# A graph attention kernel picks rows for 352 of 512 places of a chunk instead of 256

## Chip, core and metric

The kernel runs on one core of one Trainium2 chip. The metric is the device time of one execution in microseconds. Five engines work in parallel, each through its own queue in order: TensorE (PE, with its weight loads as PEld), VectorE (DVE), ScalarE (ACT), GpSimd (POOL), and SyncE (SP), which here only issues transfers.

## The reference

A graph of 6250 nodes with 64 features and 206,250 edges sorted by destination goes through three layers of transformer convolution, each edge carrying 64 features of its own:

```python
def _transformer_conv(x, src, dst, edge_attr, Wq, bq, Wk, bk, Wv, bv, We, Ws, bs):
    q = x @ Wq + bq
    kj = (x @ Wk + bk)[src] + edge_attr @ We
    alpha = sum(q[dst] * kj, -1) / sqrt(64)
    w = softmax of alpha over the edges of each dst
    agg = segment_sum(((x @ Wv + bv)[src] + edge_attr @ We) * w[:, None], dst)
    return agg + x @ Ws + bs
```

Between layers stand a relu and a layer norm, after the last a relu and a log softmax; the output is the layer norm of the input plus that result. The sources are drawn at random, so `x[src]` reads rows in no order.

## The kernel before

The edges stand in 403 chunks of 512; a chunk is 4 tiles of 128 edges, and 4 chunks make a batch. A unit is the work on one batch; a layer has 102 of them. A unit needs, for each of its 2048 edges, the row of `x` of the edge's source and the edge's own features, side by side in a buffer `feat`. TensorE transposes `feat` (`turn`, L1525), multiplies with the queries to scores (L1536, L1538), DVE takes their maximum (L1545), ACT the exponential (L1552); the weights are transposed (L1564) and sum the rows of `feat` (L1577); SP stores the parts, which are later finished to nodes, four blocks of 128 nodes at a time.

**Gathers.** A source row comes to `feat` by an indirect transfer that POOL issues, 128 rows of 64 numbers each (`gather`). Those of later units are released in order by gates: ACT copies the column of indices into a buffer (L609), and POOL's transfer reads it from there (L610).

**Picks.** A part of the rows isn't gathered but picked. All nodes stay on the chip as `halves` (each number as a rounded part and its rest). Layer 0 moves the edges inside each chunk so that certain places hold only sources out of a known range of nodes. There are 8 ranges of `BW` = 6 blocks of 128 nodes, each with 32 places in a chunk, 256 places in all: two tiles. For a pair of ranges and 8 chunks (two batches) DVE compares the keys of the places with the numbers 0 to 767 (`aim`: six comparisons of 512 columns, L1216, into `hot`), and TensorE multiplies the blocks with the ones so found (`bank`: 2 x 6 matmuls of 256 columns, L1242). ACT copies the result into `kept` (L1249), four matmuls of 64 columns per chunk-tile set turn it to rows while adding part and rest (`naturals`, L1259), and DVE copies these into `feat` (L1276, L1278). The keys come from DRAM (`key`, L1200), one load of 1024 columns, spread to all partitions, for four pairs of ranges.

`PICKED = (1, 2, 2)` says how many of the four tiles are picked in layers 0, 1 and 2. So a unit of layer 0 gathers 12 tiles, a unit of layers 1 and 2 gathers 8. The first `LEAD` = 4 batches of layer 0 are not picked at all and gather 16.

**Layer 0** does the moving while it works on units that were moved before, four chunks per unit. Every fourth unit `mark` handles 16 chunks: it finds each edge's range, counts how many of a range stand ahead of it with matmuls against a triangle (L892), takes the first 32 of each range to their places and the others to the remaining places, in their old order. These steps are separate pieces of a generator, and one is done at each quarter of a unit. Then DVE makes one-hot rows of the new positions (`hit`, L1000) and TensorE moves the features and a stamp of the source with them (products, L1012 and L1021). Tile t of the moved edges needs the first `REACH[t]` columns at most, which is why those products are narrower than 512; `mark` also checks on the chip that this holds and that every place found an edge (`few`), and a general path stands ready if not. The `index` step turns the stamps into index columns (L1058, L1061) and keys. Results go to DRAM (`eaS`, `eaP`, `toS`, `keyS`) and are read back in layers 1 and 2.

**Order in layers 1 and 2.** One iteration u issues: store the parts of u - 2, scores of u - 1, one bank, the transposes of u with the requests of u + 1 between them (`ask` and `across`: `to`, `q` and `featT` on SP), the weights of u - 1, `naturals` in every second iteration, one more bank, the sums of u - 1. The tile pools set waits: two `key` buffers, six `hot` buffers, four `feat` buffers.

## Time and profile before

| | before |
|---|---|
| time, median of 3 runs | 4249.41 us (4247.88 to 4252.58) |
| time of the profiled execution | 4238.36 us |
| its span | 4236.3 us |
| mean granted clock of TensorE | 0.872 |
| busy: PE / PEld / DVE / ACT / POOL | 81% / 61% / 73% / 49% / 71% |
| gathers, layers 1 and 2 together (L610, `feat<-x`) | 1608 with a gate, mean 1061 ns |
| gathers, layer 0 (L610, `feat<-in_x`) | 1212 with a gate, mean 1056 ns |

The busy shares are averages over stages that differ. Layer 0 runs to about 1890 us, layer 1 from 1940 to about 3050, layer 2 from about 3100 to the end. The page of the profile has no chain of waits for this execution; what sets the time is read from each engine's busy time, from its idle gaps and what ended them, stage by stage. A row of windows gives the busy time of each engine with the number of instructions, then the granted clock, the DMA share and GB/s; a row of groups gives count, busy time and mean, and after the bar the idle time just before these instructions and what ended most of it.

### The profile page before, as it was taken

To read this page: it belongs to the slowest core of one execution; us is meant where nothing else is said; L and a number is where in the kernel's file an instruction comes from. 1 tells how busy PE (TensorE), PEld (TensorE's weight loads), DVE (VectorE), ACT (ScalarE), POOL (GpSimd) and SP (SyncE) were. 2 spreads that over 40 slices of the span, in tenths; PEclk is the share of its full clock that TensorE was granted. 3 is DMA by queue.
4 is the path that set the end of the run, shared out by engine and by line. 5 is a ranking of instruction groups with operands and counts; after the bars stand their busy time and mean duration, and the time that the engine had idled before them with its cause. 6 is when DMAs were issued, how large, how long until landed. Compare 5 with 4: busy or idle time off the path is not lost.

```text
span 4236.3 us, 105299 instructions
## 1 busy us (share of the span) xinstructions
PE 3428.8 (81%) x33967; PEld 2576.5 (61%) x33967; DVE 3083.3 (73%) x8792; ACT 2090.9 (49%) x6475; POOL 3019.6 (71%) x2863
## 2 busy tenths in 40 slices
PE   5678887887888787868888888888688888888886
PEld 3445555555555555546776677766467767676774
DVE  6667777777877788856777777777567777777775
ACT  2345555455555555553455545455435555555554
POOL 5457777777776777756777777777567777777775
PEclk9889998999998999987888889889778888888887
DMA  7567777777777778854666767666546666666664
GB/s 164 153 168 201 212 199 192 202 204 199 200 212 200 195 208 214 223 158 113 161 170 172 170 162 171 160 170 169 136 111 165 161 172 163 170 165 164 164 167 105
DMA packets 749709, 737.56 MB, mean 174 GB/s; under 512 B 390960, under 2 KB 501578, under 8 KB 749150
## 3 DMA queue, kind: packets, MB, share of 16 engines
q1 hardware_dynamic: 565854, 510.70, 47.3%
q0 software_dynamic: 91264, 93.64, 12.0%
q10 hardware_dynamic: 92032, 126.38, 8.6%
q8 instruction: 276, 4.52, 0.5%
q14 instruction: 283, 2.32, 0.2%
HBM read 570.27 MB, written 160.07 MB: 172 GB/s over the span
## 4 chain that ended last, share of the span: by engine, by line


## 5 line engine op out<-in xcount | busy, mean ns | idle before, releaser
L610 POOL DMA_INDIRECT feat<-x,gate x1608 | 1705.3, 1061 | 514.3 <-issue 250.2
L610 POOL DMA_INDIRECT feat<-in_x,gate x1212 | 1279.8, 1056 | 566.9 <-ACT gate L609 263.7
L1216 DVE TENSOR_SCALAR hot<-key,rank 128x512 fp32r<-128x512 f16 x2976 | 1244.9, 486 | 112.7 <-PE ps_x L1242 87.4
L1242 PEld LDWEIGHTS ps_x<-hot,halves 128*128 128x128 f32 x4800 | 705.4, 218 | 193.8 <-DVE hot L1216 71.0
L1242 PE MATMUL ps_x<-hot,halves 128*128 128x256 f32 x4800 | 811.4, 322 | 1.4 <-DVE hot L1216 0.2
L1528 ACT COPY featT<-ps_a 64x512 f32<-64x512 f32 x1192 | 691.1, 580 | 219.3 <-PE ps_a L1525 202.3
L1525 PE MATMUL ps_a<-ident,feat 128*128 128x128 f32 x2380 | 365.1, 280 | 262.0 <-DMA feat<-x,gate 261.9
L609 ACT COPY gate<-src_b 128x1 int32<-128x1 int32 x2772 | 454.2, 191 | 94.5 <-ACT eT L1035 41.0
L1577 PE MATMUL ps_g<-feat,probT 128*32 128x128 f32 x9672 | 423.0, 326 | 86.7 <-ACT probT L1567 39.2
L1525 PEld LDWEIGHTS ps_a<-ident,feat 128*128 128x128 f32 x2380 | 274.0, 143 | 351.8 <-issue 283.8
L1249 ACT CAST kept<-ps_x 128x512 fp32r<-128x512 f32 x400 | 234.3, 586 | 414.7 <-PE ps_x L1242 412.5
L1545 DVE TENSOR_REDUCE most<-ps_s 128x1 f32<-128x512 f32 x297 | 203.8, 686 | 314.8 <-PE ps_s L1538 311.3
L1012 PE MATMUL ps_x<-hit,rest 128*64 128x512 bf16 (+3 forms) x3200 | 426.5, 356 | 0.0
L1577 PEld LDWEIGHTS ps_g<-feat,probT 128*32 128x32 f32 x9672 | 315.4, 131 | 156.6 <-ACT probT L1567 52.3
L1000 DVE TENSOR_SCALAR hit<-ruler,pos 128x512 bf16<-128x512 f16 (+3 forms) x1600 | 410.3, 326 | 0.0
L1552 ACT ACTIVATE prob<-ps_s,part 128x512 f32<-128x512 f32 x297 | 204.4, 688 | 348.9 <-PE ps_x L1242 200.3
L1538 PE MATMUL ps_s<-featT,q 128*32 128x512 f32 x2376 | 318.0, 607 | 0.0
L1012 PE MATMUL ps_x<-hit,raw 128*64 128x512 bf16 (+3 forms) x1600 | 297.0, 367 | 7.0 <-DVE hit L1000 7.0
L1567 DVE COPY probT<-ps_p 128x512 f32<-128x512 f32 x204 | 139.2, 683 | 216.8 <-PE ps_p L1564 209.3
L1564 PE MATMUL ps_p<-ident,prob 128*128 128x128 f32 (+1 forms) x1224 | 212.6, 301 | 73.2 <-ACT prob L1552 59.2
L1012 PEld LDWEIGHTS <-rest 128*64 128x64 bf16 x3200 | 197.8, 120 | 97.0 <-issue 32.4
L1564 PEld LDWEIGHTS ps_p<-ident,prob 128*128 128x128 f32 (+1 forms) x1224 | 151.4, 153 | 114.6 <-ACT prob L1552 72.7
(239 smaller groups left out, 4381.2 us busy)
## 6 DMA issues: line engine op xcount, KB each, us to landing
feat<-eaP SPq DMA_DIRECT2D x296, 512.0 KB
featT<-eaS SPq DMA_DIRECT2D x296, 512.0 KB
key<-keyS SPq DMA_DIRECT2D x248, 256.0 KB
raw<-in_ea SPq DMA_DIRECT2D x200, 256.0 KB
eaS<-eT ACTq DMA_DIRECT2D x200, 256.0 KB
eaP<-eN ACTq DMA_DIRECT2D x200, 256.0 KB
feat<-x,gate POOLq DMA_INDIRECT x1608
part<-part SPq DMA_DIRECT2D x600, 32.5 KB
```

The source lines that it names most:

```text
L609: copy(gate, index[:, i + t : i + t + 1])
L610: nc.gpsimd.indirect_dma_start(out=loaded[layer, k][:, c, t, 0], out_offset=None, in_=xts[layer][:, :], in_offset=bass.IndirectOffsetOnAxi ...
L1000: nc.vector.tensor_scalar(hit, ruler[:, : REACH[t]], self.pos[:, at : at + 1], None, ALU.is_equal)
L1012: nc.tensor.matmul(self.px[i][j * D : (j + 1) * D, : REACH[t]], self.part(i, part)[:, (j * T + t) * D : (j * T + t + 1) * D], self.hits[t, ...
L1216: nc.vector.tensor_scalar(hot, self.keys[k, t][:, 2 * i * PAIR * W : 2 * (i + 1) * PAIR * W], rank[:, h : h + 1], None, ALU.is_equal,)
L1242: nc.tensor.matmul(px[:, cols], halves[b >= EARLY][:, b - EARLY * (b >= EARLY)].rearrange("p h d -> p (h d)"), made[h][:, cols], start=(h ...
L1249: nc.scalar.copy(kept[t][:, :, 2 * i : 2 * i + 2].rearrange("p c q e -> p q c e"), px.rearrange("p (q c e) -> p q c e", q=2, e=W),)
L1525: nc.tensor.transpose(pt[:, j - js[0], t // 2], rows[:, t * D : (t + 2) * D], ident)
L1528: nc.scalar.copy(featT[:, :, :, h, :], pt[h * D : (h + 1) * D])
L1538: nc.tensor.matmul(self.p_s[rows], self.q[:, j * STRIDE : j * STRIDE + W], self.featT[:, j, :], start=False, stop=True)
L1564: nc.tensor.transpose(p_t[:, t, :n], self.prob[:n, t * P : (t + 1) * P], ident[:n, :n])
L1577: nc.tensor.matmul(p_g[rows, :].rearrange("n (h d) -> n h d", h=2), self.probT[:, t, rows], batch[:, c + j, t], start=(t == 0), stop=(t == ...
```

## The change

The places of a chunk that are picked grow from 256 to 352, in layers 1 and 2 alone: two tiles and the first 96 rows (`PART`) of the third. In layer 0 still one tile of four is picked.

- **Ranges.** There are 22 ranges of 4 blocks with 16 places each. They overlap: range w covers blocks 2w to 2w + 3. A range is made of steps of two blocks (25 `BINS`), and each edge goes to the range that has room by a running count: the steps' counts are summed, limited by the capacity so far, and turned into a shift for each step, which two scans on DVE do (L922, L924).
- **`mark`.** Ten matmuls of 128 columns are replaced by 4 of 400 columns against ones, then 14 of 400 for the counts inside each step (in four pieces, last tile first), 25 of 64 columns that add up the steps, and 10 of 16 that count the edges not placed. The pieces grow from 8 to 11; DVE reads each of these results out of PSUM. The four transposes of the old place table (`pn`) stand in the new code twice, once as a piece of their own.
- **Reach.** The columns needed by tiles 0, 1 and 2 grow to 392, 416 and 456 (the fourth always has 512).
- **Picks.** A bank now covers a pair of ranges for 16 chunks (four batches): 4 comparisons of 512 columns and 2 x 4 matmuls of 256. Layers 1 and 2 have 11 such pairs in four units, staggered so that two or three fall on each unit; layer 0 has 4. The keys of each pair come by one or two loads of their own. There are three `key` buffers and, in layers 1 and 2, two sets of `hot` buffers (`later`) instead of one.
- **Gathers.** In layers 1 and 2 a batch gathers the fourth tile of each chunk and one shared tile, `spare`, with the last 32 rows of the third tile of the four chunks: 5 transfers instead of 8. ACT copies the four parts of `spare` into `feat` (`settle`). The `naturals` of a unit are done in every iteration, for two tiles and for the 96 rows.
- **Lead.** The first 8 batches of layer 0 are not picked, instead of 4.

```diff
-BW = 6
-BINS = 2 * LB
-QUARTERS = P // W
-PAIR = 2 * LB
-NP = BINS * BW
+BW = 4
+SL = 16
+WINDOWS = 22
+SLOTS = WINDOWS * SL
+BINS = 25
+PART = SLOTS - 2 * P
+REST = P - PART
+TURN = 4
 GC = 16
 ROWS = 8
 STRIDE = W // 2
 BACK = 8
-PICKED = (1, 2, 2)
-LEAD = 4
-REACH = (288, 320, 416, CH)
+PAIRS = (P // (2 * SL), WINDOWS // 2, WINDOWS // 2)
+LEAD = 8
+REACH = (392, 416, 456, CH)
...
+    def rows_wanted(layer, k):
+
+        m = batches[k][1]
+        if not placed(layer, k):
+            return [(c, t) for c in range(m) for t in range(T)]
+        if not layer:
+            return [(c, t) for c in range(m) for t in range(1, T)]
+        return [(None, 0)] + [(c, T - 1) for c in range(m)]
+
...
+    def take(layer, k, c, t, index):
+
+        nc.gpsimd.indirect_dma_start(
+            out=spares[layer, k] if c is None else loaded[layer, k][:, c, t, 0],
+            out_offset=None,
+            in_=xts[layer][:, :],
+            in_offset=bass.IndirectOffsetOnAxis(ap=index, axis=0),
+        )
...
+    def settle(layer, k):
+
+        if layer and placed(layer, k):
+            for c in range(LB):
+                nc.scalar.copy(
+                    loaded[layer, k][PART:, c, 2, 0], spares[layer, k][c * REST : (c + 1) * REST, :]
+                )
 
...
+        those = rows_wanted(layer, k)
+        pending.extend((layer, k, c, t, k * LB + i * LB / len(those)) for i, (c, t) in enumerate(those))
...
-        nc.vector.tensor_tensor(lh, lh, ge[:, 1:], ALU.subtract)
-        yield
-        pc = ps("a")
-        sofar = pc[:, : BINS * n].rearrange("p (h c t) -> p h c t", h=BINS, t=T)
-        kinds = lh.rearrange("p h (c t) -> p h c t", t=T)
-        for t in range(T):
-            for i in range(t + 1):
-                nc.tensor.matmul(
-                    sofar[:, :, :, t], ones if i < t else tri, kinds[:, :, :, i], start=(i == 0), stop=(i == t)
-                )
...
+            kinds.rearrange("p h c t -> p h (c t)"),
+            half.unsqueeze(1).to_broadcast([P, BINS + 1, n]),
+            slab.unsqueeze(2).to_broadcast([P, BINS + 1, n]),
+            ALU.is_equal,
+        )
+        pc = ps("a")[:, : m * BINS]
+        for t in range(T):
+            nc.tensor.matmul(
+                pc.rearrange("p (c h) -> p h c", h=BINS), ones, kinds[:, :BINS, :, t], start=(t == 0), stop=(t == T - 1)
+            )
+        below, lift = [counts[:, i] for i in range(2)]
+        flat = "p c h -> p (c h)"
+        nc.vector.tensor_tensor_scan(below, carry[:, :m].rearrange(flat), pc, 0.0, ALU.mult, ALU.add)
+        yield
+        nc.vector.tensor_tensor_scan(lift, climb[:, :m].rearrange(flat), below, 0.0, ALU.add, ALU.max)
+        nc.vector.scalar_tensor_tensor(lift, below, float(SL), lift, ALU.add, ALU.subtract)
+        lift = lift.rearrange("p (c h) -> p c h", h=BINS)
+        nc.vector.tensor_reduce(few[:, 1, g : g + 1], lift[:, :, : BINS - 1], AX.XY, ALU.min)
+        nc.vector.tensor_tensor(lift, lift, shift.unsqueeze(1).to_broadcast([P, m, BINS]), ALU.add)
+        yield
+        for t in reversed(range(T)):
+            pc = ps("a")[:, : m * BINS].rearrange("p (h c) -> p h c", h=BINS)
+            for i in range(t + 1):
+                nc.tensor.matmul(pc, ones if i < t else tri, kinds[:, 1:, :, i], start=(i == 0), stop=False)
+            nc.tensor.matmul(
+                pc, ones[0:1, :], lift[0:1].rearrange("p c h -> p h c"), start=False, stop=True
+            )
+            nc.vector.tensor_tensor(kinds[:, 1:, :, t], pc, kinds[:, 1:, :, t], ALU.mult)
+            yield
+        pc = ps("a")[:, :n]
+        for h in range(BINS):
+            nc.tensor.matmul(
+                pc, same, kinds[:, 1 + h].rearrange("p c t -> p (c t)"), start=(h == 0), stop=(h == BINS - 1)
+            )
...
+        at = pc.rearrange(by, t=T)
+        for t in range(T):
+            for i in range(t + 1):
+                nc.tensor.matmul(
+                    at[:, :, t], ones if i < t else tri, kinds[:, 0, :, i], start=(i == 0), stop=(i == t)
+                )
...
+        pn = ps("a")
+        w0 = r0 // W * W
+        w = min(W, NC - k * P - w0)
+        place = pn[:, : T * w].rearrange("p (t c) -> p c t", t=T)[:, r0 - w0 : r0 - w0 + m]
+        for t in range(T):
+            nc.tensor.transpose(
+                pn[:, t * w : (t + 1) * w],
+                start[w0 : w0 + w, k * CH + t * P : k * CH + (t + 1) * P],
+                ident[w0 : w0 + w, w0 : w0 + w],
...
+            pk = pa[:LB, W : W + SLOTS]
+            nc.tensor.matmul(pk, keyc, self.to[:, :SLOTS], start=True, stop=True)
+            for t in range(1, T):
+                nc.tensor.matmul(
+                    pi[:, 1 + (t - 1) * LB : 1 + t * LB], self.to[:, t * P : (t + 1) * P], pickc, start=True, stop=True
+                )
+            for c in range(LB):
+                nc.tensor.matmul(
+                    pi[c * REST : (c + 1) * REST, 0:1], self.to[:, SLOTS : 3 * P], pickc[:, c : c + 1], start=True, stop=True
+                )
...
+            low = 0 if layer else U0
+            self.jobs = []
+            for k in range(low - TURN + 1, NT):
+                for q in range(PAIRS[layer]):
+                    if q % TURN == k % TURN:
+                        self.jobs.append((k, max(k, low), min(k + TURN, NT), q))
...
+            while self.loads and len(self.keys) < 3:
+                _, k0, k1, q = job = self.loads[0]
+                if not self.layer and not coded.issuperset(range(k0, k1)):
                     return
+                key = picks.tile([P, TURN * LB * 2 * SL], FP16, name="key", bufs=3)
+                n = LB * 2 * SL
+                while k0 < k1:
+                    m = min(k1 - k0, TURN - k0 % TURN)
+                    nc.sync.dma_start(
+                        key[:, k0 % TURN * n : (k0 % TURN + m) * n],
+                        keyS[q, k0 : k0 + m].rearrange("k c e -> (k c e)").partition_broadcast(P),
+                    )
+                    k0 += m
...
+            if not self.aims or self.aims[0] not in self.keys or len(self.hots) > (self.layer > 0):
                 return
+            job = self.aims.pop(0)
+            a, b = self.span(job)
+            pool = later if self.layer and self.aimed % 2 else picks
+            self.aimed += 1
             made = []
...
+                    block = 2 * (2 * q + w) + h
+                    assert halved[block] == self.layer
                     nc.tensor.matmul(
+                        px[:, w, a:b],
+                        halves[block >= EARLY][:, block - EARLY * (block >= EARLY)].rearrange("p h d -> p (h d)"),
+                        made[h][:, a:b, w],
...
+            found = loaded[self.layer, k]
+            for ts, tag in (((0, 1), tags[0]), ((2,), tags[1])) if self.layer else (((0,), tags[0]),):
+                n = P if ts[0] < 2 else PART
+                pn = ps(tag)[:n, : len(ts) * LB * D].rearrange("p (t c d) -> p t c d", t=len(ts), d=D)
+                for t in ts:
                     for c in range(LB):
...
-                picker.bank()
-                drip(u)
+                picker.naturals(u + 1, "mp")
+                picker.bank(u + 2)
                 close_up(3) if close else step()
-                this.turn(0, lambda: drip(u))
+                this.turn(0, lambda: drip(u, 0.5))
                 ask(layer, u + 1)
                 chunks[layer, u + 1].across()
                 this.turn(1, lambda: drip(u, 0.5))
                 close_up() if close else step()
                 line.weights(u)
                 close_up(3) if close else step()
-                if u % 2:
-                    picker.naturals(u + 1, "ms")
-                picker.bank()
+                while picker.due(u + 2):
+                    picker.bank(u + 2)
                 drip(u)
                 picker.load()
                 line.sums(u)
                 free(u, LB - 1)
+                settle(layer, u + 1)
...
-            if odd:
-                picker.bank("g")
+            picker.naturals(u + 1, "p")
+            picker.bank(u + 2, "g")
...
-            for _ in range(PICKED[layer + 1] * QUARTERS // 2):
-                picker.bank()
-            picker.naturals(0, "ms")
-            picker.bank()
+            while picker.due(0):
+                picker.bank(0)
+            picker.naturals(0, "mp")
+            settle(layer + 1, 0)
+            while picker.due(1):
```

TensorE in an iteration of layers 1 and 2, from the scores to the sums (`ps_x` is a bank, `ps_m`, `ps_s` and `ps_p` with `twice` are the naturals, `ps_a` the transposes). Before:

```order
L1538 MATMUL ps_s<-featT,q 32x512 x4
L1242 MATMUL ps_x<-hot,halves_31087 128x256 x12
L1525 MATMUL ps_a<-ident,feat 128x128 x8
L1564 MATMUL ps_p<-ident,prob 128x128 x4
L1259 MATMUL ps_m<-twice,kept_254 128x64 x4
L1259 MATMUL ps_m<-twice,kept_31088 128x64 x4
L1259 MATMUL ps_s<-twice,kept_254 128x64 x4
L1259 MATMUL ps_s<-twice,kept_31088 128x64 x4
L1242 MATMUL ps_x<-hot,halves 128x256 x12
L1577 MATMUL ps_g<-feat,probT 32x128 x16
```

After:

```order
L1605 MATMUL ps_s<-featT,q 32x512 x4
L1338 MATMUL ps_m<-twice,kept_261 128x64 x4
L1338 MATMUL ps_m<-twice,kept_32321 128x64 x4
L1338 MATMUL ps_p<-twice,kept_32322 96x64 x4
L1314 MATMUL ps_x<-hot,halves 128x256 x8
L1592 MATMUL ps_a<-ident,feat 128x128 x8
L1631 MATMUL ps_p<-ident,prob 128x128 x4
L1314 MATMUL ps_x<-hot,halves_32320 128x256 x16
L1644 MATMUL ps_g<-feat,probT 32x128 x16
```

The naturals moved from behind the weights' transposes, for two units at a time in every second iteration, to the place right behind the scores, for one unit in each; the picks are 8 and 16 matmuls instead of 12 and 12.

SP in an iteration of layers 1 and 2. Before, from one unit's `to` to the next one's:

```order
L1473 DMA to_210<-toS 6x512 x4
L1478 TENSOR_LOAD base
L1487 REGISTER_ALU
L1487 DMA q<-qq 128x80
L1504 DMA featT<-eaS 64x4x512
L1200 DMA key<-keyS 128x1024
L559 DMA feat<-eaP 128x1024
L1591 ISA
L1591 DMA part_173<-part 64x130
L1591 ISA
L1591 DMA part_174<-part 64x130
```

After:

```order
L1257 DMA key<-keyS 128x384
L1257 DMA key<-keyS 128x128
L1540 DMA to_213<-toS 6x512 x4
L1545 TENSOR_LOAD base
L1554 REGISTER_ALU
L1554 DMA q<-qq 128x80
L1571 DMA featT<-eaS 64x4x512
L1257 DMA key<-keyS 128x384
L1257 DMA key<-keyS 128x128
L559 DMA feat<-eaP 128x1024
L1658 ISA
L1658 DMA part_176<-part 64x130
```

One load of 1024 columns became loads of 512 in one or two pieces, and some of them now stand ahead of `to`, `q` and `featT`.

DVE in layer 0, at the place where a `mark` begins its counting (`hit` and `rest` belong to the moving, `most` and `part` to the scores). Before:

```order
L879 TENSOR_TENSOR ge<-src_b,edges 128x576
L885 TENSOR_TENSOR ge<-ge 128x512
L1545 TENSOR_REDUCE most<-ps_s 128x1
L1547 TENSOR_SCALAR part<-most 128x1
L982 TENSOR_TENSOR rest<-raw 128x512
```

After:

```order
L909 TENSOR_TENSOR kinds<-misc,slab 128x1664
L922 SCALAR_TENSOR_TENSOR bins<-carry,ps_a 128x400
L1612 TENSOR_REDUCE most<-ps_s 128x1
L1614 TENSOR_SCALAR part<-most 128x1
L1345 COPY feat<-ps_p 128x4x64
```

The first scan (L922) reads TensorE's result `ps_a` and stands right behind the comparison that TensorE waits for, ahead of the scores' maximum; before, nothing of `mark` read PSUM on DVE at this place, since ACT copied the counts.

259 lines of the change are left out of this document (106 added, 153 removed).

## The prediction

> **What bounds the kernel now.** I read first the busy time of each engine by stage, where layer 0 is 400 to 1800 us and layer 1 is 2100 to 3000 (columns: busy us and instructions of PE, PEld, DVE, ACT, POOL, then granted clock and DMA).
>
> ```profile
> 400.00:1800.00 1400.00, 1134.49 (x12524) 763.88 (x12524) 1092.58 (x3560) 731.88 (x2249) 1018.42 (x969) 0.92 0.77 205
> 2100.00:3000.00 900.00, 773.60 (x7544) 629.10 (x7546) 676.11 (x1654) 459.60 (x1470) 699.74 (x657) 0.88 0.68 168
> ```
>
> Then the groups of layer 1, by form, and its longest waits.
>
> ```profile
> L610 POOL DMA_INDIRECT feat<-x,gate x657 | 700.6, 1066 | 200.6 <-issue 102.1 <-ACT gate L609 43.6 <-DMA feat<-x,gate 24.1
> L1216 DVE TENSOR_SCALAR hot<-key,rank 128x512 fp32r<-128x512 f16 x996 | 416.6, 486 | 35.6 <-PE ps_x L1242 30.1 <-DVE feat L1276 0.2
> L609 ACT COPY gate<-src_b 128x1 int32<-128x1 int32 x664 | 119.1, 192 | 0.0
> L1249 ACT CAST kept<-ps_x 128x512 fp32r<-128x512 f32 x166 | 97.2, 586 | 146.3 <-PE ps_x L1242 145.4
> ...
> PE ps_a L1525 <- DMA feat<-x,gate: 103.2, 56, 5.8
> ```
>
> In layers 1 and 2 POOL never rests. Busy time and gap of its gathers are 700.6 + 200.6 = 901 us of 900, 1.372 us per gather, and the longest named part of the gap is its own issue. Eight gathers make a batch of four chunks, so a unit takes 8 x 1.372 = 10.97 us (900 / 657 x 8 = 10.96). PE, the busiest of the others, is idle 126.4 us, and 103.2 us of that is the transposes at L1525 waiting for gathered rows. DVE is busy 8.24 us of a unit (676.1 / 82.1 units), ACT 5.6.
>
> Layer 0 is another machine.
>
> ```profile
> L1000 DVE TENSOR_SCALAR hit<-ruler,pos 128x512 bf16<-128x512 f16 x320 | 99.1, 370 | 0.0
> L1000 DVE TENSOR_SCALAR hit<-ruler,pos 128x288 bf16<-128x288 f16 x324 | 73.5, 286 | 0.0
> L892 PE MATMUL ps_a<-ge,ones 128*128 128x128 f16 x120 | 22.2, 297 | 0.0
> L901 DVE TENSOR_REDUCE spare<-ge 128x64 f32<-128x512 f16 x20 | 20.6, 1028 | 0.7
> L879 DVE TENSOR_TENSOR ge<-src_b,edges 128x576 f16<-128x576 int32 x20 | 14.9, 745 | 0.0
> L1545 DVE TENSOR_REDUCE most<-ps_s 128x1 f32<-128x512 f32 x80 | 55.2, 690 | 169.0 <-PE ps_s L1538 168.9
> ```
>
> L1545 runs once a unit: 80 units in 1400 us, 17.5 us each. PE is busy 14.2 of it, DVE 13.7, and POOL needs 12 gathers, 16.5 us at 1.372. Nothing is full; PE and DVE wait for each other in turn (DVE 169 us for the scores alone), so work added to PE's queue is mostly added to the unit.
>
> **Layers 1 and 2: three gathers fewer.** A batch takes 5 gathers, 5 x 1.372 = 6.86 us of POOL. POOL stops being the bound, and the next bound sets the gain. One iteration at full clock, the same after a stall, and the queue of SP:
>
> ```profile
> 2502.40 1.06 PE L1259 MATMUL ps_m<-twice,kept 128*128 128x64 f32 x8
> 2503.29 1.06 PE L1259 MATMUL ps_s<-twice,kept 128*128 128x64 f32 x8
> ...
> 2508.51 1.03 PE L1538 MATMUL ps_s<-featT,q 128*32 128x512 f32 x8
> 2509.47 1.69 PE L1242 MATMUL ps_x<-hot,halves 128*128 128x256 f32 x12
> 2511.01 1.03 PE L1525 MATMUL ps_a<-ident,feat 128*128 128x128 f32 x8
> ...
> 2522.59 0.45 PE L1525 MATMUL ps_a<-ident,feat 128*128 128x128 f32 x1 [2.61 <-DMA feat<-x,gate]
> ...
> 2526.96 2.91 PE L1242 MATMUL ps_x<-hot,halves 128*128 128x256 f32 x12
> ...
> 2514.91 1.41 SPq L1473 DMA_DIRECT2D to<-toS  x4
> 2517.11 0.38 SPq L1487 DMA_DIRECT2D q<-qq  x1
> 2517.55 0.66 SPq L1504 DMA_DIRECT2D featT<-eaS  x1
> 2518.46 0.39 SPq L1200 DMA_DIRECT2D key<-keyS  x1
> ...
> 2521.25 2.01 SPq L1473 DMA_DIRECT2D to<-toS  x4
> ```
>
> *PE.* Now 773.6 / 82.1 = 9.42 us a unit at a granted clock of 0.88. The picks take 22 matmuls a unit instead of 24 (11 banks of 8 for four units): 12 of them start 1.54 us apart (2509.47 to 2511.01), 0.128 each, so -0.26. Turning the picks into rows takes 12 matmuls instead of 8, at 0.89 / 8 = 0.111: +0.44. That gives 9.60 us at today's clock. If the clock rose to 1.0 and all of it followed, 9.60 x 0.88 = 8.45. With the idle time that is not the gathers', (126.4 - 103.2) / 82.1 = 0.28, the bounds are 8.73 and 9.88.
>
> *DVE.* 11 comparisons instead of 12, -0.42 (416.6 / 996), and a third copy of picked rows, 96x256, at most the same: still 8.24, near PE's lower bound.
>
> *ACT.* Banks 2.75 instead of 2 (+0.44 at 0.586), four small copies of the spare rows (+0.77 at 0.192 if priced like the gates), three gates fewer (-0.54 at 0.179): 6.3 us, under the others. These copies are a new wait: they stand at the end of an iteration and wait for the spare gather, with the next exponentials and gates queued behind them. The spare is the first gather of a batch, released two iterations ahead, so I cost the wait at nothing; without that cover every late gather would stop ACT for up to the 5.8 us above.
>
> *SP.* From `to` to `to` SP's issues of one unit take 6.34 us. Keys come in 19 DMAs for four units instead of 4, 3.75 more a unit at about 0.45 with the gap before each: +1.7, about 8.0, before what finishing nodes adds. A key load also waits until the comparisons that free its buffer are done, and one now stands ahead of the next `to`, `q` and `featT`, which were ahead of it. featT is loaded an iteration before its scores, which should cover that.
>
> So the unit lands between 8.7 and 9.9 us. With PE, DVE and SP all at 8 to 9.6 and each waiting for the others, I take a value toward the upper end, **9.6 us**. Some 97 units a layer: 194 x (10.96 - 9.6) = **-264 us** (bounds -433 and -210; -154 if SP stretches it to 10.2).
>
> **Layer 0: a wider sort and a dearer rank pass.**
>
> ```profile
> 1028.64 1.67 PE L1242 MATMUL ps_p<-hot,halves 128*128 128x256 f32 x12
> 1030.24 0.33 PE L1012 MATMUL ps_x<-hit,raw 128*64 128x320 bf16 x2
> ...
> 1031.92 0.44 PE L1021 MATMUL ps_m<-hit,stamp 128*32 128x320 bf16 x8
> ```
>
> *Products.* 24 matmuls of 304 columns on average fill 1030.24 to 1031.92, 0.23 ns a column. The reaches grow by 104, 96 and 40 columns; twelve matmuls each: 12 x 240 x 0.23 = +0.66 us a unit. The stamps (0.44 us for 8 of 304: 0.18 ns) add 4 x 240 x 0.18 = +0.17. Picks: 8 matmuls instead of 12 at 1.60 / 12 = 0.133, -0.53. The index step has a few small matmuls more, +0.1.
>
> *Rank pass*, once in four units. Ten 128-column matmuls at 0.185 (22.2 / 120) go, -1.85. There come 18 of 400 columns, 35 small ones and four transposes, which stand in the code twice. No row has a 400-column one: the pick's 256 in 0.133 give 0.21, L892 scaled by columns 0.58. I take 0.21, since L892's pitch is that of its weight loads: 3.8 us. The small ones go at 0.111: 3.9. The transposes 0.5. Sum +6.3, so +1.6 a unit (upper bound 3.9: 18 x 0.58, 35 x 0.185, 0.5, less 1.85, by 4).
>
> PE's sum is +2.0 a unit (upper 4.3). DVE: hits grow by 960 columns at 0.37 ns (0.310 less 0.227 us over 224 columns), +0.36; two comparisons fewer at 0.41, -0.82; the rank pass trades 3 us of reductions and the like for a 1664-wide comparison (1.29 ns an element by L879, 2.1 us), two scans (nearest L901, 2 ns an element, 0.8 us each) and four products read out of PSUM, +0.8. Net +0.3.
>
> PE would be busy 16.2 of 17.5 us. Part of the new matmuls stands ahead of places where PE waits today; I let 0.4 of the 2.0 hide: 88 settled units x 1.6 = **+141 us** (bounds 0, if PE's 3.3 us of idle swallows it, and +380). POOL's 12 gathers, 16.5 us, stay below 19.
>
> **The edges.** At a layer's start four banks run before the first unit, now 11 narrower ones:
>
> ```profile
> 3079.48 13.01 PE L1242 MATMUL ps_x<-hot,halves 128*128 128x256 f32 x48
> ...
> 3081.38 2.53 DVE L1216 TENSOR_SCALAR hot<-key,rank 128x512 fp32r<-128x512 f16 x6 [1.03 <-PE ps_x L1242]
> ```
>
> Four banks take 13.0 us, a DVE set of six 2.5. The new ones compare 13,824 columns against 12,288, and hand over 11 times instead of 4: 0 to +8, I take +4, twice, **+8 us**. The lead of 8 batches instead of 4 makes four early batches gather 16 times; POOL still waits there, so **+5 us** (0 to +17).
>
> **Sum.** The profiled execution took 4238.4 us (span 4236.3). 4238.4 - 264 + 141 + 8 + 5 = 4128. The median of the runs shown is 11 us above the profiled one: 4139, rounded to **4140 us**.
>
> **Rivals.**
>
> *The clock follows.* After 2.6 us without work the 12 matmuls of a pick took 2.91 us instead of 1.69. If the gather waits go, these slow stretches go too, and units reach the lower bound 8.73: 194 x 2.23 = -433, with layer 0 as above 4249 - 433 + 154 = 3970 us. For it: the row above. Against it: a unit so short leaves DVE half a microsecond and SP less.
>
> The Trainium skill has the rule: its page "TensorE: Matmul & The Clock Gate", section "Why this matters for your kernels", asks for no PE gaps over about 3 us, or the clock halves. By that rule this rival is the likelier; the trace agrees in direction (2.91 against 1.69).
>
> *Slower: the rank pass crosses between PE and DVE seven times a mark*, where it crossed twice and ACT drained one of them. Each crossing in one queue order can cost DVE what its wait for the scores costs, 169.0 / 80 = 2.1 us; seven by four is +3.7 a unit. It decides once layer 0 grows by 2.85 us a unit (1.6 + 110 / 88); with half of the price the time is 4140 + 88 x 1.85 = 4300 us. For it: the waits of L1545. Against it: the steps stand a quarter of a unit apart.
>
> *SP holds layers 1 and 2 at 10.2 us*: -147 + 154, 4256 us, no change or slightly slower. For it: SP's 8.0 us plus four-unit extras; against it: it runs an iteration ahead.
>
> *The ranges do not fill* and the general path runs as well: many times slower; worked out from the inputs, every chunk fills its 352 places, so 0.01.
>
> **Chances.** Forecast 0.51 (its own range 4060 to 4215), clock 0.20, crossings 0.16, SP 0.12. About 0.2% is what a measurement of this kernel can tell. Faster 0.72, same 0.05 (half of SP's), slower 0.23. The range takes in the clock at its lower side and the crossings at half price: 3980 to 4300.
>
> **What would show it.** Right: units of 9 to 10 us in layers 1 and 2, POOL busy under 60% there, PE idle at L1525's successor nearly gone, layer 0 units near 19 us. Wrong: units under 8.8 us with clock over 0.95 (clock); layer 0 units over 20.4 us with DVE waiting on the rank pass's ps_a (crossings); units above 10 us with scores waiting for featT (SP).

## The result and the profile after

The changed kernel takes 4202.62 us (median of 4 runs, 4195.37 to 4208.52), the one before 4248.65 us in the same comparison: a ratio of 0.9891, with a 95% interval of 0.9871 to 0.9910. It is faster by 46 us, where 109 us were forecast. The range held the time; the size was wrong, and that it was not further off is luck in part: by the table below layers 1 and 2 gained 108 us less than forecast and the first ten units and the borders cost 44 us more, while the rest of layer 0 cost 73 us less.

The windows of the changed kernel (columns: busy us and instructions of PE, PEld, DVE, ACT, POOL, then granted clock, DMA share, GB/s), with the kernel before in the same stretch of layer 1 behind them:

```profile
400.00:1800.00 1400.00, 1280.76 (x12867) 716.83 (x12868) 1133.06 (x3367) 703.49 (x2144) 1008.22 (x928) 0.95 0.75 196
2200.00:3000.00 800.00, 674.78 (x7283) 548.93 (x7283) 621.80 (x1561) 515.19 (x1518) 443.37 (x391) 0.96 0.71 179
```

```profile
2200.00:3000.00 800.00, 686.45 (x6695) 557.13 (x6698) 599.61 (x1468) 405.10 (x1298) 622.34 (x584) 0.88 0.68 167
```

POOL fell from 78% to 55% busy in layer 1, as forecast, and the granted clock rose from 0.88 to 0.96. But no other engine took its place: PE is 84% busy, DVE 78%, ACT 64%, and SP, whose work is issuing, issues for 536 of the 800 us. All of them wait. The longest waits of the changed kernel in that stretch (us in total, times, longest) and the scores' small wait for `featT`, then the longest of its SP queue:

```profile
POOL spare L590 <- DVE feat L1345: 167.4, 44, 9.4
DVE hot L1282 <- DMA key<-keyS: 93.9, 51, 4.5
PEld ps_p L1631 <- ACT gate L624: 85.6, 41, 6.2
PE ps_p L1631 <- DVE feat L1345: 82.6, 39, 6.0
PE ps_s L1605 <- DMA featT<-eaS: 7.0, 6, 1.6
```

```profile
SPq L1540 <- DMA feat<-eaP: 50.8, 52, 2.5
SPq L1257 <- DVE hot L1282: 31.0, 55, 2.2
SPq L1425 <- DMA part<-part: 30.9, 10, 4.2
```

PE waits at the weights' transposes (L1631) for DVE's copy of picked rows; DVE waits for keys; keys are issued by SP. The scores hardly wait for `featT`. The instruction of the scores' maximum (L1545 before, L1612 after) runs once a unit, so its starts in the trace cut the execution into units:

| piece | before, us | after, us | measured | forecast |
|---|---|---|---|---|
| layer 0, first ten units | 242 | 277 | +35 | +5 |
| layer 0, the rest, first to last maximum | 1551 | 1619 | +68 | +141 |
| start, and the borders of the layers | 201 | 223 | +22 | +8 |
| layer 1, first to last maximum | 1111 | 1035 | -76 | -132 |
| layer 2, first to last maximum | 1101 | 1020 | -80 | -132 |
| behind the start of the last maximum | 31 | 30 | -2 | 0 |
| span | 4236 | 4204 | -32 | -110 |

Over units 5 to 94 of layer 1 the unit went from 11.00 to 10.24 us. It is not one size: 11 of these 90 units, those in which DVE begins to finish a group of 512 nodes, take 14.2 us (12.1 before), the others 9.7 (10.9 before). Layer 2 reads the same: 14.4 and 9.7.

### The profile page after: what moved, and what is told of

The parts are those of the page before. It is cut to its first block, busy times and chain, and to the rows that moved or that the text cites. A ratio compares the mean times of both kernels' runs of the same rounds, so it can differ in the third digit from the quotient of the medians.

```text
span 4204.2 us, 108531 instructions
## 1 busy us (share of the span) xinstructions
PE 3533.6 (84%) x35594; PEld 2436.6 (58%) x35594; DVE 3144.4 (75%) x8786; ACT 2305.7 (55%) x6834; POOL 2492.4 (59%) x2279
## 4 chain that ended last, share of the span: by engine, by line
## 5 line engine op out<-in xcount | busy, mean ns | idle before, releaser
L1282 DVE TENSOR_SCALAR hot<-key,rank 128x512 fp32r<-128x512 f16 (+1 forms) x2644 | 1093.3, 478 | 300.6 <-DMA key<-keyS 242.8
L590 POOL DMA_INDIRECT feat<-x,gate x816 | 896.5, 1099 | 312.0 <-ACT gate L624 105.2
L1314 PE MATMUL ps_x<-hot,halves 128*128 128x256 f32 (+2 forms) x4528 | 718.4, 311 | 1.4 <-DVE hot L1282 1.2
L1314 PEld LDWEIGHTS ps_x<-hot,halves 128*128 128x128 f32 x4528 | 637.7, 210 | 8.0 <-DVE hot L1282 4.6
L590 POOL DMA_INDIRECT spare<-x,gate x198 | 246.4, 1245 | 635.7 <-DVE feat L1345 393.6
L1061 PE MATMUL ps_x<-hit,rest 128*64 128x512 bf16 (+3 forms) x3200 | 463.4, 372 | 0.0
L1631 PE MATMUL ps_p<-ident,prob 128*128 128x128 f32 (+1 forms) x1224 | 209.1, 298 | 267.5 <-DVE feat L1345 206.2
L624 ACT COPY gate<-src_b 128x1 int32<-128x1 int32 x2130 | 360.4, 192 | 100.5 <-ACT eT L1084 37.0
L1644 PE MATMUL ps_g<-feat,probT 128*32 128x128 f32 x9672 | 352.0, 286 | 33.7 <-DVE probT L1634 24.4
L1322 ACT CAST kept<-ps_x 128x512 fp32r<-128x512 f32 (+3 forms) x566 | 313.5, 576 | 78.0 <-PE ps_x L1314 72.7
L1631 PEld LDWEIGHTS ps_p<-ident,prob 128*128 128x128 f32 (+1 forms) x1224 | 146.8, 151 | 317.0 <-ACT gate L624 223.0
L1644 PEld LDWEIGHTS ps_g<-feat,probT 128*32 128x32 f32 x9672 | 268.7, 114 | 103.5 <-DVE probT L1634 30.7
L1061 PE MATMUL ps_x<-hit,raw 128*64 128x512 bf16 (+3 forms) x1600 | 308.2, 382 | 0.0
L1338 PEld LDWEIGHTS ps_m<-twice,kept 128*128 128x128 f32 x1600 | 196.2, 193 | 167.9 <-issue 167.9
L1652 ACT COPY part<-ps_g 128x128 f32<-128x128 f32 (+1 forms) x309 | 83.2, 269 | 363.6 <-PE ps_g L1644 350.7
```

What stands on the lines that cost most here:

```text
L590: nc.gpsimd.indirect_dma_start(out=spares[layer, k] if c is None else loaded[layer, k][:, c, t, 0], out_offset=None, in_=xts[layer][:, :], ...
L624: copy(gate, index[:, i : i + 1])
L1061: nc.tensor.matmul(self.px[i][j * D : (j + 1) * D, : REACH[t]], self.part(i, part)[:, (j * T + t) * D : (j * T + t + 1) * D], self.hits[t, ...
L1282: nc.vector.tensor_scalar(hot[:, a:b].rearrange("p k w e -> p (k w e)"), self.keys[job][:, a * 2 * SL : b * 2 * SL], rank[:, h : h + 1], None,
L1314: nc.tensor.matmul(px[:, w, a:b], halves[block >= EARLY][:, block - EARLY * (block >= EARLY)].rearrange("p h d -> p (h d)"), made[h][:, a: ...
L1322: nc.scalar.copy(kept[t][:, a:b, at : at + 2 * SL].rearrange("p k (w e) -> p w k e", w=2), px[:, :, a:b])
```

## Experiments: layers 1 and 2

**Is it SP's queue?** Two edits take issues away from SP and leave bytes and the other engines' work as they are.

```diff
-                for j in range(m):
-                    nc.sync.dma_start(self.to[j * n : (j + 1) * n, :], toS[self.k, j * W : j * W + n])
+                nc.sync.dma_start(
+                    self.to[: m * n, :], toS[self.k].rearrange("(j w) e -> j w e", w=W)[:m, :n, :]
+                )
```

> The changed kernel with the four loads of to on SP (6 rows each) made one load of 24 rows. Takes three of about twelve issues of a unit from SP, about 0.5 us each, 1.5 us a unit, in all layers. Theory 1 (SP's queue is the bound in layers 1 and 2): the units of layers 1 and 2 shrink by 0.4 to 0.9 us until PE's 8.6 us busy and DVE's 7.9 stand in the way, 4203 - 194 x 0.65 = about 4080 (4030 to 4130). Theory 2 (DVE's and ACT's order sets the unit, SP only follows): no more than 20 us less.

Measured: 4050.82 us, 0.9522 of before (0.9501 to 0.9543). Layers 1 and 2 took 972 and 955 us, units of 9.64 and 9.59.

```diff
-                    m = min(k1 - k0, TURN - k0 % TURN)
+                    m = k1 - k0
```

> The changed kernel with each load of keys in layers 1 and 2 as one transfer of 512 columns where it was two pieces. The columns of a wrapped load then stand in the wrong order, so the rows picked are those of other places: the output isn't the reference's, the bytes and all other work are the same. Takes 2 of 4.75 key issues of a unit from SP, about 1.0 us a unit. Theory 1: 4203 - 194 x (0.3 to 0.7) = 4065 to 4145 us. Theory 2: no more than 20 us less. If the waits of the comparisons for keys (93.9 us in 800) are a matter of landing time and not of SP's queue, they stay as they are.

Measured: 4042.09 us, 0.9516 (0.9492 to 0.9540); layers 1 and 2 took 953 and 949 us. (The edit reaches the key loads of layer 0 too; layer 0 took 9 us less in the profiled execution.) DVE's waits for keys, which the expectation names as a test of the landing time, did not stay: in the 700 us from 2200 they fell from 86 us to 31. Three issues fewer, or two, gave 0.6 to 0.8 us a unit each; the first result lies inside what theory 1 expected, the second past its lower end. SP's rows of the changed kernel, and that of the one load in its place, show what an issue costs (ns min/median/max):

```profile
L1540 SPq DMA_DIRECT2D to<-toS x312: 256/280/1157, 2205.9 to 2997.6; - x156
L1545 SPq TENSOR_LOAD <-base x78: 516/537/697, 2208.9 to 2997.9; - x78
```

```profile
L1539 SPq DMA_DIRECT2D to<-toS x82: 752/770/1694, 2199.5 to 2986.1; - x82
```

Four issues of 0.28 us became one of 0.77, but the register load behind it now takes 0.75 us instead of 0.54 (medians). So SP issues for 6.8 us a unit in both kernels (536 us for 79 units, 560 us for 82), and yet the unit lost 0.6 us: what went is waiting, not issuing. The semaphores in the trace show what SP waits for. Its transfers signal their landing on eight semaphores in turn (all 1110 transfers of the 800 us), and 1079 of them are issued only when their own semaphore was signalled, that is when the transfer eight before them has landed. SP stands still for 172 us in pieces of over 0.1 us; 115 us of that end at such a landing, 73 us of them in front of `to`, one of whose loads often stands eight behind the 512 KB load of `feat`. With one load of `to` it is 37 of 154 us, and before the change 44 of 337. The changed kernel issues 14.1 transfers a unit, the one before 10.5, the one with one load of `to` 11.0. This is read from the traces; no run changed the number of semaphores, or moved a transfer to another queue.

The same edit in the kernel before:

> The kernel before with the four loads of to made one. SP is relieved by the same three issues a unit as in the changed kernel, where that was worth 152 us. Theory: before the change layers 1 and 2 are set by POOL's eight gathers, so SP's relief is worth nothing there: 4235 to 4255 us. If SP's queue was part of the bound already: 4200 or less.

Measured: 4260.8 us, 1.0021 (1.0005 to 1.0037), 6 us above the expected range and, if anything, slower. Where POOL sets the unit, SP's relief is worth nothing. So it is the change that put SP's queue on the path. Whether SP has time to spare also shows in how long its key loads wait for DVE to free a buffer: 31.0 us in the changed kernel (above), but in the one before

```profile
SPq L1200 <- DVE hot L1216: 143.1, 45, 8.5
```

**What would the gathers alone have given?**

```diff
         p = picked(layer, k)
+        those = [(c, t) for c in range(batches[k][1]) for t in range(p, T)]
+        if p == 2:
+            those = [(0, 2)] + [(c, 3) for c in range(LB)]
...
+            if t == 2 and picked(layer, k) == 2:
+                nc.gpsimd.memset(loaded[layer, k][:, 1:, 2, 0], 0.0)
```

> The kernel before, with only 5 of the 8 gathers of a batch in layers 1 and 2 (three tiles are zeroed by one memset on POOL instead, so their rows are left out and the output isn't the reference's). All else stands as before: the relief of POOL alone, without the dearer picks, the key loads and the new layer 0. By the prediction's sum a unit is then set by PE's 9.42 us at most: 9.4 + 0.3, about 4249 - 194 x 1.3 = 4000 us. If the finishing units hold SP here too, they add about 5 us each, 24 times: 4120 us. If POOL was not what set layers 1 and 2, 4220 or more.

Measured: 3923.38 us, 0.9227 (0.9207 to 0.9246), better than its sum. Layers 1 and 2 lost 327 us together (953 and 932 us, units of 9.47 and 9.30). The sum had PE's 9.42 us at a clock of 0.88; without the gather waits the clock is higher and PE's share of a unit smaller:

```profile
2200.00:2900.00 700.00, 619.58 (x6509) 497.76 (x6502) 571.88 (x1430) 380.50 (x1062) 406.13 (x434) 0.94 0.70 180
```

Of the 327 us that the three gathers are worth, the changed kernel kept 156; what else it brings gave 171 back. That the added work alone did not cost this is shown by the fastest version below, which does all of it and takes 915 and 899 us in the two layers.

**Keys laid out for one transfer.** Layer 0 writes a batch's keys to the row of the windows that will use them, sorted by pair modulo four, so that each load is contiguous.

```diff
-    keyS = dram.tile([WINDOWS // 2, NT, LB, 2 * SL], FP16, name="keyS")
+    keyS = dram.tile([TURN * 3, NT // TURN + 1, TURN, LB, 2 * SL], FP16, name="keyS")
...
-            nc.scalar.dma_start(keyS[:, k].rearrange("q c e -> c q e"), key)
...
+            nc.scalar.dma_start(
+                keyS[: 3 * (r + 1), j + 1, r].rearrange("q c e -> c q e"), key[:, : 3 * (r + 1)]
+            )
+            if r < TURN - 1:
+                nc.scalar.dma_start(
+                    keyS[3 * (r + 1) :, j, r].rearrange("q c e -> c q e"), key[:, 3 * (r + 1) :]
+                )
```

> The changed kernel with the keys laid out in DRAM so that each load of 512 columns in layers 1 and 2 is one transfer with the right columns: layer 0 writes a batch's keys to the rows of the windows that use them (on ACT, two stores in three of four units instead of one, the pairs reordered in ACT's copy). By the run with one transfer and wrong columns, layers 1 and 2 lose 155 us; layer 0 gets 0.75 small transfers a unit more on ACT, 0 to 20 us. Expected 4050 us (4035 to 4080). If the writing of keys holds layer 0's index step, 4080 or more.

Measured: 4074.48 us, 0.9583 (0.9558 to 0.9609), in the expected range. Layers 1 and 2 took 953 us each, as in the run with one transfer before; layer 0 gave 32 us of it back in the profiled execution. (In the three later versions with the same layer 0 it is 11 to 16 us.)

**The finishing units.** A finishing step loads the part sums (`both`, L1425) behind the stores of the last parts. In the changed kernel ACT copies the sums of a unit, and SP stores them and loads them back (timelines: start, duration in us; the first row is ACT's, the others SP's):

```profile
2487.14 0.27 ACT L1652 COPY part<-ps_g 128x128 f32<-128x128 f32 x1 [0.33 <-PE ps_g L1644]
```

```profile
2495.18 0.32 SPq L559 DMA_DIRECT2D feat<-eaP  x1
2495.76 1.20 SPq L1658 DMA_DIRECT2D part<-part  x2
2501.29 0.95 SPq L1425 DMA_DIRECT2D both<-part  x2
2502.34 0.46 SPq L1257 DMA_DIRECT2D key<-keyS  x1
2502.88 1.33 SPq L1540 DMA_DIRECT2D to<-toS  x4
```

and DVE and ACT at the same place:

```profile
2505.14 0.17 DVE L1436 TENSOR_TENSOR mm<-sk,both 128x8 f32<-128x8 f32 x1 [2.45 <-DMA both<-part]
2505.62 0.68 DVE L1612 TENSOR_REDUCE most<-ps_s 128x1 f32<-128x512 f32 x1
2505.74 0.21 ACT L1440 ACTIVATE mm<-mm 128x8 f32<-128x8 f32 x1 [6.78 <-DVE mm L1439]
2507.31 0.41 DVE L1345 COPY feat<-ps_p 96x256 f32<-96x256 f32 x1
```

SP stands still for 4.3 us between the stores and the loads. The sums that it stores at 2495.76 were ready at 2487.41: SP is most of a unit behind, not ahead. The semaphores show that the loads wait until the stores have landed. The Trainium skill's page "DMA: Bandwidth & Descriptors", section "Anatomy of one DMA — SWDGE (gpsimd) path", says for another queue that most of a transfer's fixed cost is the confirmation of its last write. What the 4.3 us on SP's own queue consist of, no run here shows. Then DVE waits 2.45 us for the loads, with the scores' maximum and the copies of picked rows behind it, and ACT 6.78 us with the exponential behind it.

First the whole step a unit later, so that its loads are ahead of the next stores:

```diff
-            line.store()
             if layer:
                 close_up()
+            line.store()
```

> The changed kernel (4202.6 us), with one line moved in layers 1 and 2: the step that finishes a group of 512 nodes starts one unit later, so that its two loads of the part sums (both<-part) stand on SP ahead of the next stores and not behind the stores they need. Theory 1: in the changed kernel SP's queue is full, and about twelve times a layer it stands still until the stores of the parts have landed (4.3 us) before it can issue these loads, with to, q, featT and the keys queued behind them; such a unit takes about 5.5 us more than the others (14.9 against 9.4). Then about 2 x 12 x 5.5 = 130 us can go at most, since some of the wait may only move; expected 4080 to 4130 us, the long units of 14 to 16 us gone. Theory 2: the long units are the finishing work itself, on DVE and ACT, wherever it starts: within 20 us of 4203.

Measured: 4243.83 us, 0.9989 (0.9971 to 1.0007): 41 us slower than the change. Neither theory expected a loss. The waits of SP show that the standstill changed sides; now the stores wait for the loads:

```profile
SPq L1658 <- DMA both<-part: 50.3, 14, 6.9
```

Then the loads alone, half a unit later, behind `featT`:

> The changed kernel; in layers 1 and 2 the two loads of a finishing step (both<-part) stand on SP behind featT of the same unit, half a unit away from the stores ahead of them and from the stores behind them; the finishing step starts its arithmetic at the same place as before. Theory: starting a whole unit later only moved the wait (the stores then stood still for the loads, 50.3 us in 800 where the loads had waited 30.9), so the price of a finishing unit is SP standing still beside the stores, on either side. Then the long units shrink from 14.9 to some 11 us: 4203 - 24 x 4 = about 4105 us (4070 to 4140), and SP waits for neither. Rival: the finishing work on DVE and ACT makes the long units: within 20 us of 4203.

Measured: 4227.23 us, 0.9943 (0.9927 to 0.9960), 25 us slower than the change: a second miss. SP's standstill fell (21.6 us for 9), but the loads now came too late for DVE:

```profile
DVE mm L1436 <- DMA both<-part: 67.9, 9, 8.9
```

So a third edit: the loads where the change has them, the arithmetic one unit later.

```diff
             for _ in range(3):
                 yield
+        elif layer and not at_end:
+            yield
```

> The changed kernel; in layers 1 and 2 the loads of a finishing step stay where they are, but its first arithmetic (on DVE, L1436) comes one unit later. The two runs that moved the loads came out 41 and 25 us slower, and the later the loads, the longer DVE waited for both<-part at that line (30.4 us for 9 steps in the changed kernel, 67.9 with the loads behind featT), with the scores' maximum and the copies of picked rows queued behind it. Theory: that wait of DVE, not SP's standstill, makes the long units; with a unit of distance the loads have landed and the units of 14 to 16 us fall to about 11: 4203 - 24 x 4 = 4105 us (4080 to 4140). Rival: SP's standstill ahead of to, q and featT makes them: within 25 us of 4203.

Measured: 4183.88 us, 0.9830 (0.9795 to 0.9866). That is 19 us, little beside the spread of its runs (4165.59 to 4196.78), and the finishing units only fell from 14.2 to 13.3 us in layer 1 and from 14.4 to 14.0 in layer 2: the rival's range. In this kernel, where SP is behind, taking one of the two waits away alone does not shorten the long unit to 11 us.

**All together.** With one load of `to`, one load per set of keys and the loads of a finishing step behind `featT`:

> The changed kernel with all three: one load of to, one load per set of keys, the finishing loads behind featT. If SP's queue is what held layers 1 and 2, the gains stop where the next bound stands: the units of the kernel before with five gathers (9.3 us, where its SP had few keys to load) or lower, 4203 - 194 x (10.15 - 9.3) = 4040 at least, and with the finishing wait gone 9.0: 3980 (3930 to 4030). If each of the three relieved the same standstill, no less than 4030.

Measured: 4030.45 us, 0.9479 (0.9453 to 0.9504). The gains overlap; units other than the finishing ones take 8.7 and 8.6 us in the two layers, finishing ones still 14.7, with DVE waiting 58.6 us for `both` in nine of them (in 700 us of layer 1). With the arithmetic a unit later as well:

> The changed kernel with one load of to, one load per set of keys, the finishing loads behind featT and their arithmetic a unit later. The run with the first three came out at 4030 us with finishing units of 14 to 15 us and others of 8.8. If DVE's wait for both<-part makes the long units: 4030 - 24 x 4 = 3935 us (3910 to 3970). If the finishing work itself does: 4030 (4010 to 4040).

Measured: 3970.56 us, 0.9331 (0.9299 to 0.9363). It is the fastest kernel here that leaves nothing out, 280 us below the one before (4250.55 in its own comparison) and 232 below the change. Finishing units fell to 9.8 and 10.6 us, and DVE's wait for `both` is gone. The distance between loads and arithmetic, worth 19 us in the changed kernel, is worth 60 here. The two steps are not quite the same: here the loads also stand half a unit later, which by itself had cost 25 us. SP has time to spare again and waits for DVE's key buffers (700 us):

```profile
SPq L1265 <- DVE hot L1291: 125.6, 113, 3.1
```

Next to none of its idle time now ends at the landing of the transfer eight before (0.2 of 148 us, with 9.3 transfers a unit). And with the loads moved back behind the stores:

> As the fastest version so far (3970.6 us), but with the finishing loads where the change has them, right behind the stores, so that SP stands still until these have landed; the arithmetic still comes a unit later. If that standstill costs where SP has room, 4 us in each of 24 finishing units: 4040 to 4070 us. If the distance between loads and arithmetic did it all: within 15 us of 3970.

Measured: 3998.73 us, 0.9411 (0.9380 to 0.9441), 28 us slower, about 1 us a finishing unit, less than the 4 expected. SP stands still in both versions: here 37.6 us for the stores to land, in the fastest 25.6 us for the loads (in 700 us of layer 1). In the profiled executions the whole loss lies in layer 2 (937 us after 899; layer 1 took 914 and 915); why, is not shown.

The windows of the fastest version in layer 1:

```profile
2200.00:2900.00 700.00, 642.09 (x7228) 522.66 (x7227) 618.18 (x1551) 515.13 (x1516) 474.17 (x387) 1.00 0.82 204
```

PE is 92% busy at a clock of 1.00, DVE 88%. Counted by the maximum's instruction alone (the count in brackets is its own), 700 us of layer 1 hold 64 units before the change, 69 after it, 72 with one load of `to` and 77 in the fastest version:

```profile
2200.00:2900.00 700.00, 43.81 (x64) 0.88 0.69 168
```

```profile
2200.00:2900.00 700.00, 46.94 (x69) 0.96 0.72 180
```

```profile
2200.00:2900.00 700.00, 49.08 (x72) 0.96 0.76 190
```

```profile
2200.00:2900.00 700.00, 52.50 (x77) 1.00 0.82 204
```

## Experiments: layer 0

The wider products alone, in the kernel before (`REACH = (392, 416, 456, CH)`):

> The kernel before with the products of layer 0 as wide as in the changed one (392, 416, 456 columns instead of 288, 320, 416 in tiles 0 to 2); the sort stays as it is. One term of the prediction alone: PE +0.83 us and DVE +0.36 us a unit, in 98 units. If four fifths of it are added to the unit, as the prediction took: +0.66 x 88 = +58 us, 4310 us. If it goes into PE's idle time in the ratio that the whole change showed (units of layer 0 grew 0.74 us for 2.2 us more of PE): +25 us, 4275 us.

Measured: 4276.94 us, 1.0062 (1.0041 to 1.0084), +26 us: 0.27 us a unit for 0.83 us of PE (by its trace PE is busy 0.77 us more a unit). By the profiled executions the unit grew by 0.54 us; between kernels whose layer 0 is the same code, layer 0 differs by up to 29 us from one profiled execution to another, 0.3 us a unit, so the two figures do not contradict each other.

The longer lead alone, in the kernel before (`LEAD = 8`):

> The kernel before with the first 8 batches of layer 0 not picked instead of 4: four early units gather 16 tiles instead of 12 and have no picks. The changed kernel's first ten units took 36 us more than before, where the prediction had 5. If the lead makes them longer: +25 to +36 us, 4275 to 4287 us. If the new rank pass, with its eleven pieces, makes them longer: 0 to +8 us, 4250 to 4258 us.

Measured: 4238.48 us, 0.9970 (0.9954 to 0.9986). It makes nothing longer; its first ten units took 238 us against 242. With the wider products these took 243. So the 35 us of the first ten units come from neither alone; what is left is the rank pass and the picks, and that was not shown directly.

The counting matmuls of the rank pass doubled, in the changed kernel:

```diff
                 nc.tensor.matmul(pc, ones if i < t else tri, kinds[:, 1:, :, i], start=(i == 0), stop=False)
+                nc.tensor.matmul(pc, nils, kinds[:, 1:, :, i], start=False, stop=False)
```

> The changed kernel with the ten counting matmuls of 400 columns (L933) of each rank pass issued twice, the second time against zeros, which adds nothing to the counts. By the trace they take 93.1 us in 78 units, 1.2 us a unit. If PE's idle time takes most of it, as it did with the wider products (0.54 us for 0.83), the units of layer 0 grow by 0.4 to 0.8 us: 4203 + 98 x 0.6 = 4260 us (4240 to 4280). If DVE's wait behind these matmuls (100.0 us at L937 in 1400) is on the path, they grow by the whole 1.2 us or more: 4320 us (4300 and above).

Measured: 4291.79 us, 1.0102 (1.0067 to 1.0137), 89 us more than the change: 0.9 us a unit in 98 units, for 1.2 us of PE, between the two expectations and nearer to the second. DVE's wait behind them rose from 100.0 us in 77 pieces to 154.0 in 72 (the first row is the change, the second this run):

```profile
DVE kinds L937 <- PE ps_a L934: 100.0, 77, 4.2
```

```profile
DVE kinds L940 <- PE ps_a L937: 154.0, 72, 7.1
```

The repeated transposes taken out:

> The changed kernel without the four transposes of the place table that stand in its rank pass a second time. PE 4 x 0.22 = 0.9 us less in four units, 0.2 us a unit: 0 to 20 us less in layer 0, 4183 to 4203 us. If a piece of the rank pass costs by its crossing and not by its matmuls, nothing.

Measured: 4201.45 us, 0.9890 (0.9860 to 0.9920), no difference from the change.

## Why the prediction was wrong in size

**Right: what bound before, and that the bound goes.** POOL set layers 1 and 2. With five gathers and nothing else changed they lose 327 us, and one load of `to`, worth 152 us after the change, is worth nothing before it.

**Wrong: "SP ... about 8.0, before what finishing nodes adds" and "it runs an iteration ahead".** This is the step that failed: SP's issuing was sized right, but its waits stood at nothing. In the 800 us of layer 1 SP issues for 536 us, and the steps of under 0.1 us between issues add 92: 628 / 79 = 8.0 us a unit, as forecast. On top of that it stands still for 172 us, 2.2 us a unit: 115 us of it until the transfer eight before has landed, most of the rest between the stores and the loads of finishing units and for key buffers. So SP was not ahead; it stored sums 8.3 us after they were ready. What came late by this were the keys (DVE waited 93.9 us for them) and the part sums, not `featT`: the scores waited 7.0 us for it, so the prediction's "which should cover that" held, and of its two signs for this rival, units above 10 us and scores waiting for `featT`, only the first came. The forecast unit was 9.6 us; the measured one is 10.24, the size of the rival "SP holds layers 1 and 2 at 10.2 us", which had 0.12. That rival ended at 4256 us only because layer 0 was sized too dear beside it. For finishing nodes the sum had TensorE's work, as a part of the average unit, and nothing for the waits around it: 11 of 90 units at 14.2 us instead of 9.7 are 0.55 of the 0.64 us that a unit is over the forecast. (The -154 us that the sum names for a unit of 10.2 us is a slip: 194 x 0.76 is 147, as the rival has it. The forecast does not rest on it.) Rightly put at nothing was the wait of ACT's copies for the spare gather: 7.4 us in the 800.

**A hit for the wrong reason.** Ordinary units do take 9.7 us, next to the 9.6 forecast. But the 9.6 were PE's work at a clock of 0.88, and PE is now busy 674.78 / 78 = 8.65 us of a unit at a clock of 0.96; the rest is waiting, and much of it goes when SP is relieved: with one load of `to` and one per set of keys the same units take 8.6 to 8.9 us.

**The rival of the clock was half right.** The clock rose, to 0.96, and to 1.00 in the fastest version, whose ordinary units take 8.9 and 8.7 us in layers 1 and 2, at the lower bound of 8.73. That it rose because waiting went is not so simple: in 700 us of layer 1 PE is idle 103 us before the change and 108 after it, with 8 and 9 gaps of over 3 us. The trace gives the clock in stretches at full and at half speed. Before the change there are 23 stretches at half speed in these 700 us, 174 us long together, and in the 6.8 us ahead of 16 of them PE had no gap of 3 us; the change leaves 11, 55 us long, 9 of them behind gaps of 3.5 to 6.0 us, 8 of these in the finishing units; the fastest version has none. The Trainium skill's rule in "TensorE: Matmul & The Clock Gate" (section "Why this matters for your kernels"), that gaps of over about 3 us cost clock, agrees with the 9 of 11 after the change, but not with the 16 of 23 before it. The gain in clock could not show in the change's time, because SP's queue, and not PE, came next.

**Layer 0: the sum was right, the share that hides was not.** PE's busy time rose from 14.2 to 1280.76 / 78 = 16.4 us a unit, +2.2 for the forecast +2.0. That the sum fits is luck, since its terms do not:

```profile
L917 PE MATMUL ps_a<-kinds,ones 128*128 128x400 f16 x80 | 44.8, 731 | 66.8 <-DVE kinds L909 63.6 <-ACT eN L1096 3.2
L933 PE MATMUL ps_a<-kinds,ones 128*128 128x400 f16 x120 | 52.0, 523 | 0.0
L933 PE MATMUL ps_a<-kinds,tri 128*128 128x400 f16 x78 | 41.1, 527 | 0.7
L934 PE MATMUL ps_a<-bins,ones 1*128 1x400 f16 x78 | 65.8, 843 | 0.0
```

These matmuls of 400 columns take 203.7 / 78 = 2.6 us a unit, where the sum had 3.8 / 4 = 0.95: they take 203.7 / 356 = 0.57 us each, and of the two prices that it weighed, 0.21 us and 0.58, it took the lower. Against that the products (L1012, L1021; after the change L1061, L1070) grew by 0.2 us a unit instead of 0.83 (693.2 us for 80 units, 692.0 for 78), and the sums of layer 0 (L1577, L1644) took 0.4 less, on which the prediction did not count.

The unit grew by 0.70 (17.35 to 18.05 over 85 settled units) and not by 1.6. "I let 0.4 of the 2.0 hide" gave one share to all of it. By the medians of the runs above two thirds of the wider products hide (0.27 of 0.83) and one quarter of the rank pass's matmuls (0.9 of 1.2); the first share is less sure, one third by the profiled executions. The shares do not add up to the whole either: with them, 0.27 for the products, three quarters of 1.6 for the rank pass and -0.4 for picks and index give 1.0 and not 0.70. Where the rest hides is open. At the place where DVE used to wait for scores it hardly waits any more; that wait fell from 168.9 us to

```profile
DVE most L1612 <- PE ps_s L1605: 27.2, 48, 1.3
```

and in all DVE is idle 267 us of the 1400, after 307.

**The rival of the crossings** named the right place: DVE does wait for the rank pass (100.0 us at L937, 48.5 at L922, 30.7 at L945). But these waits stand where others stood, since DVE's idle time did not grow, and the unit's growth of 0.70 us stayed far below the 2.85 us at which the rival would have decided.

**The edges** were too cheap: +22 us at start and borders instead of +8, +35 us in the first ten units instead of +5. The term blamed for the latter, the lead, was the wrong one; with the counting matmuls doubled these ten units take 286 us after 277, so the rank pass is at least a part of it.

## What to carry to other kernels

An engine that only issues transfers is an engine: count its issues a unit, add register loads, the waits between issues and how many transfers may be on the way at once, and ask whether it is ahead in time and not only in program order. When a bound is taken away that every unit shared, look for the units that are longer than the others; a uniform bound hides them, and they come out once it is gone. Two waits in one chain can each look like the cause and each be worth little alone, so test them together as well as apart.

## What was not expected of the hardware

One load of 24 rows costs SP 0.77 us to issue where four of 6 rows cost 4 x 0.28, but the register load behind it went from 0.54 us to 0.75 and SP's issuing stayed at 6.8 us a unit; what fell was its waiting for earlier transfers to land, from 115 us in 800 to 37. A queue that issues for 67% of the time (536 of 800 us) can still be what the others wait for. A load that follows stores to the same table held SP for 4.3 us, and stores that follow loads of it for up to 6.9 us. TensorE's granted clock in layer 1 does not go by the busy share: it is 0.88 at 86% busy before the change and 0.96 at 84% after it. After the change its stretches at half speed are few and stand behind gaps: 8 of the 11 in 700 us begin within 2.5 us of the eight finishing steps, where PE stood still for 3.8 to 6.0 us. Before it most stand behind shorter gaps, and why these cost clock there and not after the change is open.
